# A four-layer graph transformer on one core: layernorm taken apart and run inside the product ahead of it

## The chip, the cores and the metric

The kernel runs on one core of a Trainium2 chip. Its time is the device time of that core for one launch, in microseconds; three runs are given by their median. One further execution was taken by the hardware profiler, and every duration of a single step below comes from that one. The engines are called as in the profile: PE multiplies matrices (PEld loads its stationary operand), DVE is the vector engine, ACT the scalar engine, POOL is GpSimd, and SP sends for most of the transfers.

## The reference, cut to what matters

```python
# x: 512 tokens x 768 features, float32; edges: 16384 (src, dst)
for layer in range(4):
    xn = layernorm(x)                       # (x - mean) / sqrt(var + eps)
    x = x + gnn[layer](xn, edges) + mix[layer](xn)
    x = x + ffn[layer](layernorm(x))
# gnn: graph attention with 8 heads, then 1 (layers 0, 1); graph convolution (2, 3)
# mix[0](xn): y = layernorm(xn) * g1 + b1;  xn = xn + performer(y) @ proj_w + proj_b
#             y2 = layernorm(xn) * g2 + b2; xn + gelu(y2 @ fc1_w + b) @ fc2_w + b   (3072 wide)
# mix[1](xn): linear attention on layernorm(xn) * g + b, then @ w_proj
# mix[2](xn): linear attention, then @ Wo;   mix[3](xn): as mix[0] with linear attention, eps 1e-8
# ffn: 0: mixture of 8 experts of 192 and a shared one; 1: small classifier on 6 tokens with an MLP;
#      2: 3 experts of 1536 and a shared one; 3: 8 experts of 192, 64 tokens each
```

So layernorm over 768 features stands behind a sum into the residual and ahead of the next matrix product some dozen times.

## The kernel before, in words

The tokens are split into four tiles of 128 (`NT` = 4, index t), the features into six chunks of 128 (`KC` = 6, index k). A matrix that a product contracts over features is held feature-major (`xT`), and the residual `x`, and in layers 0 and 3 also `xn`, token-major. A scheduler turns the program into one instruction list for each engine, and decides when a buffer of a pool is handed over.

Every large product is done by Strassen's method in Winograd's form: seven half-size products, each on a half of the tokens and features. The sums of the left operand (`SplitA`, four of them, `s[1]` to `s[4]`) are made on DVE by `all_sums` (L391), where the third, `s[3]` of the code's numbering or buffer `st[2]`, is made on POOL in three pieces (L396); for hidden layers POOL makes all of them (L382 to L385). The differences of the weight (`SplitB`, `t[1]` to `t[4]`) are made on POOL by twelve operations, L411 to L414 for each of three k. `ready` (L398) loads a weight and splits it. The room for weights is a pool of two buffers, later two pools: `w_tile` (L121) takes every third tile from the last pool, the rest from the first, whichever buffer there comes free first. The room for differences has two buffers as well.

`strassen_add` (L543) adds a product into the residual. For each of two halves m of the token tiles it forms banks x, y and z in PSUM and adds them to token tiles m and 2 + m as they come (L583 `add_part`, L821 `add`). The second half of the work for m is `held` and run by `flush`, so that it lies behind the next stage's first products. With `fresh` the product a22·t4 is formed early, in bank x. Which tiles are finished when is fixed by this order: token tiles 0 and 2 first, then 1 and 3.

After the sum a layernorm follows (`normed` L276, `layernorm` L210, `layernorm_chunk` L217), tile by tile in the order 0, 2, 1, 3: two `bn_stats` (L221), an aggregate (L222), a square root on ACT (L225), a reciprocal (L226), three steps of a Newton correction (L229 to L231), and the apply over 768 features (L232). When tiles 0 and 1 are there, `half(0)` of `transposer` (L234) turns them feature-major: twelve PE transposes (L246) and six times two evacuations on ACT and DVE (L202, L204, L254, L257). The second half and `all_sums` are called by the next product once its first parts are under way.

In layer 0 the performer's projection (`proj`) and the first weight of the MLP (`up`, fc1) are made ready while attention runs; `residual_and_mlp` (L817) does the projection with `strassen_add(As, wp, add, True)`, the norm y2, and `mlp` (L793), whose five groups go up and down. Before the performer the normed input is read back from DRAM, normed again, given the projection's bias on POOL and written to a DRAM copy `kept_xn0`. The shared expert of layer 0's mixture is done after the last group's weights are asked for. In layer 1 a tile called `room` is held in one of the weight buffers while the attention heads run, and the last graph attention, whose edges are made by `last_edges` (L1363), lies behind the projection `w_proj`.

## Time and profile before

| what | value |
|---|---|
| median of three runs | 3228.47 us (3226.35 to 3235.73) |
| profiled execution | 3229.27 us, its span 3227.6 us |
| PE busy | 3094.6 us, 96% of the span, 12097 matmuls and transposes |
| DVE, POOL, ACT busy | 1524.1, 1461.4, 637.7 us |
| share of 16 DMA engines | 22.7% |
| mean clock granted to PE | 0.981 |

The profiled execution is 0.8 us above the median and its span leaves 1.7 us around it, so sums made in the profile carry over. The time of an engine's group in the profile is followed by the idle time just ahead of it and by what ended that idle time, written as an arrow with engine, buffer and line. In a timeline row the columns are start, duration, engine, line, operation, out<-in, shape and count; the bracket at its end is the idle time before it and its releaser. A float32 matmul appears as two rows. Idle time of an engine that is not the bound costs nothing.

### The profile page before, as it was taken

The page shows a single profiled execution, that of the slowest core. Times are in us where ns is not written, and L with a number is a line of the kernel's source. Part 1 is how long each engine was busy: PE and PEld are TensorE (multiplying, and loading weights), DVE is VectorE, ACT ScalarE, POOL GpSimd, SP SyncE. Part 2 cuts the span into 40 slices and gives each one's busy share as a digit, 9 for nine tenths or more (in the row PEclk, how much of TensorE's full clock was granted, in tenths as well). Part 3 has the DMA queues.
Part 4 walks back from the last instruction along what each step waited for, and adds up shares of the span by engine and source line. Part 5 has one row for each costly group of instructions (what it writes and reads, how often), then busy time and mean ns, then how long its engine had stood idle before and what let it go on. Part 6 is the DMA issues. An engine that isn't in the chain of part 4 may idle for free.

```text
span 3227.6 us, 32219 instructions
## 1 busy us (share of the span) xinstructions
PE 3094.6 (96%) x12097; PEld 2066.8 (64%) x12097; DVE 1524.1 (47%) x3433; ACT 637.7 (20%) x1268; POOL 1461.4 (45%) x1560
## 2 busy tenths in 40 slices
PE   8999999999999999999998999999999999999999
PEld 3445555555765776765684357777777775677755
DVE  7574444445446324446676535433333336453241
ACT  0132222222252110201441212100000001121101
POOL 0344444445225564464534254355555557355520
PEclk9999999999999999999999999999999999999999
DMA  3021221112202122321111422122222222131221
GB/s 111 14 79 69 69 69 69 69 69 108 88 30 93 59 101 76 108 94 68 45 67 68 119 82 98 59 88 88 89 88 88 89 86 84 70 108 59 89 97 59
DMA packets 92837, 255.23 MB, mean 79 GB/s; under 512 B 9905, under 2 KB 14897, under 8 KB 91530
## 3 DMA queue, kind: packets, MB, share of 16 engines
q1 hardware_dynamic: 92682, 253.18, 22.7%
q8 instruction: 95, 1.56, 0.2%
q14 instruction: 60, 0.49, 0.0%
HBM read 244.23 MB, written 8.93 MB: 78 GB/s over the span
## 4 chain that ended last, share of the span: by engine, by line
PE 81%; DVE 9%; POOL 4%; issue 3%; ACT 1%; DMA 0%; SPq 0%; POOLq 0%; DVEq 0%; ACTq 0%
PE ps L461 39%; PE ps L553 22%; PE ps L751 4%; PE ps L614 3%; PE ps L302 3%; DVE st_u L664 2%; PE ps L922 1%; PE ps L909 1%; PE ps L246 1%; DVE edge_w L637 1%; DVE edge_w L639 1%; POOL tw L411 1%; POOL w L412 1%; POOL tw L413 1%; PE ps L1711 1%
## 5 line engine op out<-in xcount | busy, mean ns | idle before, releaser
L411 POOL TENSOR_TENSOR tw<-w 128x384 f32<-128x384 f32 x246 | 249.9, 1025 | 1094.0 <-PE ps L461 324.0
L461 PE MATMUL ps<-sx,tw 128*128 128x256 f32 x1188 | 304.8, 381 | 3.3 <-DVE sx L393 2.3
L461 PE MATMUL ps<-sx,w 128*128 128x256 f32 x1188 | 293.2, 383 | 0.8 <-DVE room L1264 0.8
L553 PE MATMUL ps<-tw,sx 128*128 128x384 f32 x720 | 252.3, 489 | 9.6 <-POOL tw L413 5.8
L412 POOL TENSOR_TENSOR w<-w 128x384 f32<-128x384 f32 x246 | 253.0, 1036 | 8.5
L413 POOL TENSOR_TENSOR tw<-w 128x384 f32<-128x384 f32 x246 | 252.4, 1033 | 9.5
L414 POOL TENSOR_TENSOR tw<-w,tw 128x384 f32<-128x384 f32 x246 | 250.3, 1024 | 9.9
L553 PE MATMUL ps<-w,sx 128*128 128x384 f32 x720 | 252.5, 486 | 0.0
L461 PEld LDWEIGHTS ps<-sx,w 128*128 128x128 f32 x1188 | 227.4, 192 | 34.5 <-DVE room L1264 1.5
L461 PEld LDWEIGHTS ps<-sx,tw 128*128 128x128 f32 x1188 | 226.4, 191 | 35.4 <-PE ps L461 3.4
L553 PEld LDWEIGHTS ps<-tw,sx 128*128 128x128 f32 x720 | 136.1, 190 | 106.5 <-POOL sx L383 8.0
L583 DVE TENSOR_TENSOR x<-x,ps 128x384 f32<-128x384 f32 x218 | 116.1, 552 | 185.9 <-PE ps L553 185.7
L553 PEld LDWEIGHTS ps<-w,sx 128*128 128x128 f32 x720 | 136.8, 190 | 92.8
L504 DVE TENSOR_TENSOR st_u<-st_p,ps 128x256 f32<-128x256 f32 (+1 forms) x127 | 57.1, 450 | 271.9 <-PE ps L461 271.9
L477 ACT COPY st_p<-ps 128x256 f32<-128x256 f32 (+1 forms) x127 | 50.2, 395 | 667.5 <-PE ps L461 665.6
L461 PE MATMUL ps<-xfT,w 128*128 128x256 f32 x720 | 180.2, 389 | 0.1
L461 PE MATMUL ps<-tw,sx 128*128 128x384 f32 x456 | 166.7, 499 | 14.0 <-DVE st_u L499 6.0
L751 PE MATMUL ps<-edge_wT,h 128*128 128x512 f32 x384 | 168.0, 594 | 8.7 <-DVE edge_wT L204 8.7
L499 DVE TENSOR_TENSOR st_u<-st_p,ps 128x256 f32<-128x256 f32 (+1 forms) x127 | 57.1, 450 | 246.8 <-PE ps L461 143.0
L461 PE MATMUL ps<-w,sx 128*128 128x384 f32 x456 | 160.5, 489 | 1.0 <-DVE ps L505 1.0
L461 PEld LDWEIGHTS ps<-xfT,w 128*128 128x128 f32 x720 | 140.2, 195 | 24.2 <-ACT st_p L477 0.3
L553 PE MATMUL ps<-w,hid 128*128 128x384 f32 x432 | 143.1, 487 | 0.0
(460 smaller groups left out, 5093.3 us busy)
## 6 DMA issues: line engine op xcount, KB each, us to landing
w<-in_L_gnn_W SPq DMA_DIRECT2D x60, 768.0 KB, 6.2
w<-in_L_mix_fc_w SPq DMA_DIRECT2D x48, 768.0 KB, 6.9
row<-in_rows SPq DMA_DIRECT2D x39, 384.0 KB, 3.6
w<-in_L_mix_qkv_w SPq DMA_DIRECT2D x18, 768.0 KB, 7.3
w<-in_L_ffn_w SPq DMA_DIRECT2D x18, 768.0 KB, 6.7
w<-in_L_ffn_routed_gate SPq DMA_DIRECT2D x18, 768.0 KB, 6.0
w<-in_L_ffn_routed_up SPq DMA_DIRECT2D x18, 768.0 KB, 5.9
w<-in_L_ffn_routed_down SPq DMA_DIRECT2D x18, 768.0 KB, 6.0
```

The lines of the kernel that those rows point to most:

```text
L302: T.matmul(ps, parts[k][:, ts(t, P)], w_of(k)[:, ts(c, HC)], start=k == 0, stop=k == n - 1)
L411: G.tensor_sub(tt[:, 0, k], b22[:, k], b12[:, k])
L412: G.tensor_sub(b12[:, k], b12[:, k], b11[:, k])
L413: G.tensor_sub(tt[:, 1, k], b22[:, k], b12[:, k])
L414: G.tensor_sub(tt[:, 2, k], b21[:, k], tt[:, 1, k])
L461: T.matmul(bank, l, r, start=start and k == 0, stop=stop and k == KC // 2 - 1, skip_group_check=True)
L499: V.tensor_add(b["u2"], b["p1r"], b["y"])
L553: T.matmul(b[name], l[:, k, ts(m, P)], r[:, k, :], start=start and k == 0, stop=k == KC // 2 - 1, skip_group_check=True)
L583: V.tensor_add(x[:, t, ts(j, HC)], x[:, t, ts(j, HC)], ps)
L614: T.matmul(acc[t], oh[:, 1, ts(t, P)], oh[:, 0, :], start=j == 0, stop=j == EC - 1)
L664: V.scalar_tensor_tensor(junk, h[:, t, :], 1.0, r, op0=ALU.mult, op1=ALU.mult, accum_out=sc[:, t : t + 1])
L751: T.matmul(ps, h[:, s, ts(f, P)], wT[:, s, :], start=s == 0, stop=s == NT - 1)
```

## The change: what it does

The class `Norm` takes the place of `normed`. Its `part(t, c)` makes the `bn_stats` of half a token tile, and after the second half of a tile `finish(t)` runs the rest of the chain with the same steps as before; `first()` and `rest()` transpose the two halves. `strassen_add` gets a parameter `then`. With it the products come in another order, in which token tiles 0 and 1 receive their last add first, every final add of a half tile is followed by its `bn_stats`, and nothing is held back; the transposes of the first half follow the last product. The `fresh` form is gone from it. The norm is given to `strassen_add` at the projection of layers 0 and 3 (y2), at the last `down` product of both MLPs (the norm of the expert layers), at the end of the experts of layers 0 and 2, and at layer 2's `Wo`. The adds of layer 1's graph attention and classifier call `part` as well, and performer's norm runs tile by tile inside the last `aggregate`.

`all_sums` makes its third sum on DVE in one operation. The bias of the projection is added to `xn` on POOL after the features of the keys instead of before the copy, and the copy is dropped. The shared expert of layer 0 is split: its first products stand between the first `strassen_add` and the second half of group 1, its last ones ahead of the last `strassen_add`. The weight buffers are given out in a fixed turn (a, b, later c, a, b), and a tile that is `held`, layer 1's `room`, leaves the turn until it is given back.

```diff
-    wpools = []
-    taken = [0]
-    def open_weights(bufs):
-        p = tc.tile_pool(name="weights", bufs=bufs, side="right")
-        wpools.append((p, p.__enter__()))
-        taken[0] = 0
-    open_weights(2)
-    def w_tile(name="w"):
-        taken[0] += 1
-        i = len(wpools) - 1 if taken[0] % 3 == 1 else 0
-        return wpools[i][1].tile([P, KC * D], FP, tag="w", name=name)
+    wpools, turns = [], []
+    def open_weights(names):
+        p = tc.tile_pool(name="weights", bufs=1, side="right")
+        wpools.append(p)
+        pool = p.__enter__()
+        turns[:0] = [(pool, n) for n in names]
+    open_weights("ab")
+    def w_tile(name="w", held=None):
+        pool, n = turn_ = turns.pop(0)
+        (turns if held is None else held).append(turn_)
+        return pool.tile([P, KC * D], FP, tag="w" + n, name=name)
...
-    def layernorm(src, dst, eps, order=range(NT), then=None):
-        for t in order:
-            layernorm_chunk(src, dst, eps, t)
-            if then:
-                then(t)
-    def layernorm_chunk(src, dst, eps, t):
...
+    class Norm:
+        def __init__(self, src, name, eps, gain=None, bias=None, sums=True, inplace=False):
+            self.src, self.eps = src, eps
+            self.n = src if inplace else token_major(name)
+            self.T, self.split, self.half = transposer(name + "T", gain, bias, sums)
+            self.st, self.seen = {}, {}
+        def part(self, t, c):
+            if t not in self.st:
+                self.st[t] = tiny(2, 6, name="ln_st")
+                self.seen[t] = 0
+            V.bn_stats(self.st[t][:, c, :], self.src[:, t, ts(c, HC)])
+            self.seen[t] += 1
+            if self.seen[t] == 2:
+                self.finish(t)
+        def chunk(self, t):
+            for c in range(2):
+                self.part(t, c)
+        def finish(self, t):
+            eps = self.eps
+            mv = tiny(2, name="ln_mv")
+            V.bn_aggr(mv, self.st[t].rearrange("p a b -> p (a b)"))
...
+            V.tensor_scalar(self.n[:, t, :], self.src[:, t, :], mean, rs, op0=ALU.subtract, op1=ALU.mult)
+        def first(self):
+            self.half(self.n, 0)
+        def rest(self):
+            self.half(self.n, 1)
...
-    def normed(src, name, eps, gain=None, bias=None, sums=True, order=(0, 2, 1, 3)):
-        xn = token_major(name)
-        dst, split, half = transposer(name + "T", gain, bias, sums)
-        if not sums:
-            layernorm(src, xn, eps, order, by_halves(xn, half))
-            return xn, dst
-        layernorm(src, xn, eps, order, lambda t: half(xn, 0) if t == 1 else None)
-        return xn, dst, split, lambda: half(xn, 1)
...
         def all_sums(self):
             self.eng.tensor_add(self.st[:, 0], self.a21, self.a22)
             self.eng.tensor_sub(self.st[:, 1], self.st[:, 0], self.a11)
+            self.eng.tensor_sub(self.st[:, 2], self.a11, self.a21)
             self.eng.tensor_sub(self.st[:, 3], self.a12, self.st[:, 1])
-            for k in range(KC // 2):
-                G.tensor_sub(self.st[:, 2, k], self.a11[:, k], self.a21[:, k])
...
-    def strassen_add(A, B, add, fresh=False):
+    def strassen_add(A, B, add, then=None):
         banks = [{}, {}]
@@ -555,25 +556,44 @@
             tick()
             return b[name]
+        def plain():
+            for n in range(2):
+                ps = product(n, "x", A.a11, B.b11, True)
+                for i, j in ((0, 1), (1, 0), (1, 1)):
+                    add(2 * i + n, j, ps)
+            for n in range(2):
+                add(n, 0, product(n, "x", A.a12, B.b21, False))
+                if then:
+                    then(n, 0)
+        if then:
+            plain()
+            flush()
+            for m in range(2):
+                add(m, 1, product(m, "y", A.s[2], B.t[2], True))
+            for m in range(2):
+                add(2 + m, 1, product(m, "z", A.s[1], B.t[1], True))
+                add(m, 1, product(m, "z", A.s[4], B.b22, False))
+                then(m, 1)
+            for m in range(2):
+                add(2 + m, 1, product(m, "y", A.s[3], B.t[3], False))
+                then(2 + m, 1)
+            for m in range(2):
+                add(2 + m, 0, product(m, "y", A.a22, B.t[4], False))
+                then(2 + m, 0)
+            return
         def chunk(m):
             def first():
                 if m == 0:
-                    for n in range(2):
-                        ps = product(n, "x", A.a11, B.b11, True)
-                        for i, j in ((0, 1), (1, 0), (1, 1)):
-                            add(2 * i + n, j, ps)
-                    for n in range(2):
-                        add(n, 0, product(n, "x", A.a12, B.b21, False))
-                    if fresh:
-                        for n in range(2):
-                            add(2 + n, 0, product(n, "x", A.a22, B.t[4], True))
+                    plain()
                 add(m, 1, product(m, "y", A.s[2], B.t[2], True))
                 add(2 + m, 1, product(m, "z", A.s[1], B.t[1], True))
                 add(2 + m, 1, product(m, "y", A.s[3], B.t[3], False))
             def second():
                 add(m, 1, product(m, "z", A.s[4], B.b22, False))
-                add(2 + m, 0, banks[m]["y"] if fresh else product(m, "y", A.a22, B.t[4], False))
+                add(2 + m, 0, product(m, "y", A.a22, B.t[4], False))
...
+    def performer_norm():
+        y = token_major("y")
+        nc.sync.dma_start(y, raw_xn)
+        return Norm(y, "y", 1e-5, "m0_g1", "m0_b1", inplace=True)
+
+    def performer_values(n):
 
         B = ready(qkv[:, 2 * D :])
-        xn = token_major("xn")
-        nc.sync.dma_start(xn, raw_xn)
-        _, _, ys, rest = normed(xn, "y", 1e-5, "m0_g1", "m0_b1")
-        add_row_to(xn, row("m0_p"))
-        nc.sync.dma_start(kept0, xn)
+        n.first()
...
-        values(ys, B, row("m0_v"), lambda t, c: va[c][:, t, :, 0:3:2, :], rest)
+        values(n.split, B, row("m0_v"), lambda t, c: va[c][:, t, :, 0:3:2, :], n.rest)
...
+                if norm and n < NT:
+                    norm.chunk(n)
...
-                strassen_add(pending[1], down, add_part)
+                n = None
+                if g == 4:
+                    if after:
+                        after()
+                    n = norm()
+                strassen_add(pending[1], down, add_part, n and n.part)
             else:
                 early()
             pending = g, sums
-        flush()
-
-    def residual_and_mlp(As, wp, eps, g2, b2, w1, f1, w2, f2, func, xn, after=None, kept_in=None):
+        n.first()
+        return n
...
-        strassen_add(As, wp, add, True)
-        flush()
-        _, _, ys, rest = normed(xn, "y2", eps, g2, b2)
+        n = Norm(xn, "y2", eps, g2, b2)
+        strassen_add(As, wp, add, n.part)
+        n.first()
...
         kT = performer_features(ys, 1)
+        add_row_to(xn, row("m0_p"))
...
+        stages = up_part(0)
+        next(stages)
+        pending = next(stages)
+        stages = up_part(1)
+        next(stages)
+        strassen_add(pending, ready(a["L0_ffn_w2"][:D, :]), add_part)
+        flush()
...
         pg, pu = feature_product(wi, xfT, 0), feature_product(wi, xfT, P)
         glu(hid[:, 0, :], pg, pu)
         ps = feature_product(wi, xfT, 2 * P)
         glu(hid[:HD, 1, :], ps[:HD], ps[HD:])
-        strassen_add(pending[1], last, add_part)
-        flush()
+        pending = next(stages)
+        last = ready(a["L0_ffn_w2"][D:, :])
+        gat_w1 = ready(a["L1_gnn_W1"])
+        n1 = Norm(x, "xn", 1e-5)
         token_product([hid[:, 0, :], hid[:HD, 1, :]], lambda k: (w2a, w2b)[k], add_to_x)
+        strassen_add(pending, last, add_part, n1.part)
+        n1.first()
...
-        room = w_tile("room").rearrange("p (i n) -> p i n", n=N)
+        holding = []
+        room = w_tile("room", holding).rearrange("p (i n) -> p i n", n=N)
...
+                nf.part(t, c)
+        turns.extend(holding)
...
-    strassen_add(As, wo, add_part, True)
-    flush()
-    _, xfT, xs, rest = normed(x, "xf", 1e-5)
+    nf = Norm(x, "xf", 1e-5)
+    strassen_add(As, wo, add_part, nf.part)
+    nf.first()
```

## The prediction

> **What bounds the kernel now.** I read the page's busy times first, then its chain of waits, then TensorE's groups with the idle time ahead of each, then the timeline of single stages.
>
> ```profile
> PE 3094.6 (96%) x12097; PEld 2066.8 (64%) x12097; DVE 1524.1 (47%) x3433; ACT 637.7 (20%) x1268; POOL 1461.4 (45%) x1560
> PE 81%; DVE 9%; POOL 4%; issue 3%; ACT 1%; DMA 0%; SPq 0%; POOLq 0%; DVEq 0%; ACTq 0%
> ```
>
> TensorE (PE) is the bound: it idles 3227.6 − 3094.6 = 133 us in all. No other engine is half busy, so a change that removes no product can win only from these 133 us and from matmuls that run slowly around them. Where the idle time lies (last columns: what it waited for):
>
> ```profile
> L246 PE MATMUL ps<-ident,xn 128*128 128x128 f32 x120 | 16.1, 280 | 4.8 <-DVE xn L232 4.2 <-DVE ln_nw L229 0.5
> L246 PE MATMUL ps<-ident,y 128*128 128x128 f32 x96 | 15.6, 313 | 14.8 <-DVE y L232 13.4 <-DVE ln_rs L231 1.4
> L246 PE MATMUL ps<-ident,xf 128*128 128x128 f32 x96 | 14.1, 292 | 12.9 <-DVE xf L232 12.9
> L553 PE MATMUL ps<-w,aT 128*128 128x384 f32 x96 | 36.8, 525 | 5.4 <-DMA w<-in_L_mix_w_proj 4.8 <-DVE xn L821 0.5
> L461 PE MATMUL ps<-tw,sx 128*128 128x384 f32 x456 | 166.7, 499 | 14.0 <-DVE st_u L499 6.0 <-POOL sx L396 5.7 <-DVE sx L393 2.2
> ```
>
> The transposes (L246) behind a layernorm wait 32.5 us for its last step, the apply L232. One such stage, layer 3's y2, on PE and then in windows (PE, PEld, DVE, ACT, POOL busy; granted clock; DMA):
>
> ```profile
> 2886.20 4.03 PE L553 MATMUL ps<-w,sx 128*128 128x384 f32 x12
> 2893.64 0.88 PE L246 MATMUL ps<-ident,y 128*128 128x128 f32 x6 [3.41 <-DVE y L232]
> 2896.25 1.54 PE L246 MATMUL ps<-ident,y 128*128 128x128 f32 x6 [1.74 <-DVE y L232]
> 2897.59 7.43 PE L461 MATMUL ps<-y2T,w 128*128 128x256 f32 x24
> 2906.69 2.86 PE L461 MATMUL ps<-y2T,tw 128*128 128x256 f32 x12 [0.36 <-DVE y2T L254]
> 2910.39 1.53 PE L461 MATMUL ps<-sx,tw 128*128 128x256 f32 x6 [0.84 <-DVE sx L393]
> ```
>
> ```profile
> 2882.00:2890.00 8.00, 8.00 (x26) 4.56 (x24) 5.44 (x13) 0.24 (x2) 4.74 (x6) 1.00 0.00 0
> 2890.00:2898.00 8.00, 2.86 (x14) 2.19 (x14) 7.59 (x25) 1.81 (x7) 8.00 (x8) 0.80 0.82 288
> 2898.00:2906.00 8.00, 8.00 (x35) 6.73 (x35) 1.03 (x3) 3.90 (x8) 5.17 (x6) 0.77 0.02 7
> 2906.00:2911.00 5.00, 3.80 (x19) 2.88 (x17) 4.80 (x8) 0.97 (x3) 2.09 (x3) 1.00 0.00 0
> ```
>
> The product's last add is followed by statistics, a chain of small steps and two applies; PE stands 6.35 us in four gaps. Then the clock is 0.80 and 0.77, so a gap costs twice. Counting each matmul's excess over the median of its group (here 3.6 us), this stage loses 9.95 us. Such losses, gaps and excess, over all of PE (us): start of layer 0: 3.6; performer y 8.8; layer 0's y2 9.1; xf 6.7; start of layer 1: 11.3; its projection 15.2; its xf 4.5; start of layer 2: 7.0; its xf 8.9; start of layer 3: 8.0; second norm .3; y2 9.95; last xf 2.3. Sum 95.7. The rest of the 133 (routers, sorting, layer 1's edges) is untouched.
>
> The 15.2 are not a norm:
>
> ```profile
> 1722.15 1.41 SPq L156 DMA_DIRECT2D w<-in_L_mix_w_proj  x3
> 1726.95 4.54 PE L553 MATMUL ps<-w,aT 128*128 128x384 f32 x8 [4.83 <-DMA w<-in_L_mix_w_proj]
> 1736.33 0.91 PE L553 MATMUL ps<-tw,sx 128*128 128x384 f32 x2 [2.58 <-POOL tw L413]
> 1740.50 1.65 PE L553 MATMUL ps<-tw,sx 128*128 128x384 f32 x2 [3.26 <-POOL tw L413]
> ```
>
> The weight is sent for at 1722.15, when the buffer before it is let go; PE waits for it, then twice for POOL's differences, and runs slowly for 4.5 us.
>
> **The change, part by part.**
>
> *Norm by parts.* A product in `strassen_add` is three matmuls of 0.672 us, 14 products about 28.3 us. In the new order tokens 0 and 1 get their last add (z, s4·b22) before ten more matmuls, 6.7 us. Their chain there: add .55, bn_stats .56, aggregate .2, square root .29, reciprocal .15 and three small steps of .2, with the hand-overs about 1.55, two applies at the slow 1.30: 5.3 us, under 6.7. So the first twelve transposes follow the last matmul directly. Tokens 2 and 3 take the same 5.3 us after the end; ahead of PE lie 12 transposes (1.5) and nine to twelve matmuls of 0.448 (4.0 to 5.4), 5.5 to 6.9. What is left is the wait for DVE's sums of the transposed half (two sums of .94 ahead of the wanted one): 1.5 to 1.8 a stage. No bn_stats is added; where `fresh` stood 18 adds replace 20, 1.1 us less DVE. DVE's work beside the product is 18 × .46 + 8 × .5 + 4 × 2.2 = 21 us of 28.3, so it keeps up.
>
> *all_sums.* Three POOL operations of .72 become one on DVE of about .95. Two prices speak: on DVE it comes first and can hold the next sums by .95; on POOL it sat behind row adds (5.7 us of waits in the group above). At the start of layer 2 POOL's is the gap of 4.17; it goes.
>
> *Rule against trace, ports.* The apply took 1.30 and L392 1.39 beside POOL work, .68 and .95 apart from it. The Trainium skill, SBUF — State Buffer, "Who interferes with whom", says that a VectorE instruction with two SBUF inputs, or a copy or tensor_scalar in a 2-port mode, is locked out for a whole GpSimd operation. That speaks against laying the norm beside the split of the next weight (1.0 us an operation). By the rule in full, four applies would wait 4 × 1.0 more a stage, 44 us over eleven; by the rows, +.62, already in the 5.3. I take the rows.
>
> *Rule against trace, clock.* The same skill, TensorE: Matmul & The Clock Gate, Part 1, gives half clock after one idle window of about 3.4 us until one busy window: an estimate of 1.7 us lost a stage. The rows show 2.5 to 3.7. With gaps cut to 1.8 us both say that the loss goes; by the rule the sum would be about 10 us smaller over ten stages. I take the rows.
>
> *Two stages with a new wait.* At layer 2's xf and layer 3's y2 the a22 products stood early as cover; now s2·t2 follows the first products, and DVE does four sums (3.7 us) ahead of the adds that free the banks. 1.7 to 2.5 us; I take 2.5.
>
> *Buffers, layer 0.* Before, the projection's weight was sent for at 892.64 and split at 899 to 912; fc1's at 997.96, split from 1003.96. With fixed turns the projection gets the slot that is free last. Its 12 split operations (1.0 each) then begin near 1004 and alternate with fc1's: PE stands about 3.3 + 1 us for differences and 1.5 for the transfer, and loses 2.5 by the clock. That is +7.5 to 8.3 and eats what y2 gains (9.1 − 1.8). Net 0, bounds −3 (it fits) and +4.
>
> *Buffers, layer 1.* The projection gets q's slot, done near 1675: transfer 6 us, split 12 us, ready about 1694, 28 us ahead of need. 14 of the 15.2 go; bound 10, if the row adds on POOL come first.
>
> *The rest.* Start of layer 1: the second norm waits 1 to 3 us more behind reduces while one reduce fewer stands before L499; gain 3, bounds 0 and 7. The moved shared expert issues the same matmuls; gat_w1 now loads after it, 7 + 12.4 us beneath a 28.3 us product. Dropping the round trip of xn saves two 1.5 MB transfers nobody waits for. The row add to xn (8 × .96 = 7.7 us) moves to POOL's idle 10.49 us ahead of 894.80. These cost nothing while that cover stands; without it 1 to 3 us each.
>
> **Sum.** Gains: 3 + 6.2 + 0 + 4.9 + 3 + 14 + 1 + 5.5 + 4.6 + 6.3 + 5.6 + .3 + 1.5 = 55.9. The profiled execution took 3229.27 (span 3227.6 and 1.7 around it), .8 above the median 3228.47. So 3229.3 − 55.9 = 3173.4, on the median 3172.6. I say 3174.
>
> **The rivals.**
> 1. Waits come back (.22). If sums first and slow applies leave 3.4 us a stage, not 1.7, PE still drops its clock: 1.7 + 1.0 back at each of ten stages, 27 us: about 3201. For: DVE is 7.59 of 8 busy in the bad window. Against: the chain fits by 1.4 us.
> 2. Only the buffers pay (.08): the scheduler reorders the adds so that the norm still comes last. 3228.5 − 14 = 3214. Against: the instruction order of the changed kernel, laid beside the old, keeps the adds and statistics as written.
> 3. Slower (.05): fixed turns. A weight must now take its own slot, not whichever comes free first. There are 246 / 3 = 82 split weights; each late one stops PE. To cross to slower by .3% it must cost (55 + 9.7) / 82 = .8 us a weight. At 1.0 each: 3256. For: the layer 0 case. Against: elsewhere the order of the transfers hardly moves, and the product of 28 us hides 18 to 20 us of load and split.
> 4. It does nothing, gains at stages given back at layers 0 and 1 (.03): 3226.
>
> **How the numbers follow.** Forecast .62, own range 3155 to 3192 (its bounds: layer 1's start ±4, layer 0 ±4, the projection −4, three quarters of a microsecond at ten stages). The range 3150 to 3206 adds most of rival 1. A measurement here tells .3%, 9.7 us, from no change: the forecast, rival 1 and rival 2 are faster: .92; same .03; slower .05.
>
> **What would show it.** In the profile after: PE idle near 98 us (35 of the gain is gaps) and busy about 3074 (21 is slow matmuls); L246's waits for L232 from 32.5 to under 8; windows after a product's end at clock .95 or more; no gap on the layer 1 projection and its issue near 1675 less the time won; gaps for L413/L414 of 3 us in layer 0's projection. Wrong, if the transposes still wait over 3 us, if L553 waits for weights at many places, or if DVE is over 55% busy.

## The result, and the profile after

| | median (range), us | profiled execution, its span |
|---|---|---|
| before | 3228.64 (3226.35 to 3235.73) | 3229.27, 3227.6 |
| after | 3206.02 (3205.90 to 3208.21) | 3206.01, 3204.3 |

The ratio is 0.9928, with a 95% interval of 0.9911 to 0.9945. (A fourth execution of the kernel before moves its median from 3228.47 to 3228.64.) The change wins 22.6 us where 55 were forecast: it is faster, by less than half of what the sum said, and 3206.02 lies at the upper end of the range 3150 to 3206.

The page after, first the busy times, then the chain that ended last by engine:

```profile
PE 3082.3 (96%) x12087; PEld 2060.9 (64%) x12097; DVE 1540.6 (48%) x3442; ACT 635.4 (20%) x1266; POOL 1430.0 (45%) x1515
PE 83%; DVE 10%; POOL 3%; issue 2%; ACT 1%; DMA 0%; SPq 0%; POOLq 0%; DVEq 0%; ACTq 0%
```

PE's idle time went from 133 to 3204.3 − 3082.3 = 122 us and its busy time from 3094.6 to 3082.3: 11 us of gaps and 12 of busy time were won, where 35 of gaps and 21 of slow matmuls were forecast. So 24 of the 33 us that are missing are gaps that stayed or came. PE's groups after (last columns: idle time ahead, and what ended it):

```profile
L461 PE MATMUL ps<-sx,tw 128*128 128x256 f32 x1188 | 306.7, 383 | 9.5 <-DVE sx L394 8.5 <-DVE st_u L499 1.0
L554 PE MATMUL ps<-tw,sx 128*128 128x384 f32 x720 | 253.7, 490 | 13.2 <-DVE sx L394 5.3 <-POOL sx L384 4.1 <-POOL tw L413 3.8
L554 PE MATMUL ps<-tw,aT 128*128 128x384 f32 x48 | 19.2, 554 | 5.3 <-DVE xn L854 5.3
L267 PE MATMUL ps<-ident,xn 128*128 128x128 f32 x120 | 15.5, 273 | 1.2 <-DVE xn L247 1.2
L267 PE MATMUL ps<-ident,xf 128*128 128x128 f32 x96 | 12.9, 283 | 3.8 <-DVE xf L247 3.8
L267 PE MATMUL ps<-ident,y 128*128 128x128 f32 x96 | 12.1, 273 | 0.0
L461 PE MATMUL ps<-w,xnT 128*128 128x384 f32 x312 | 112.9, 501 | 9.4 <-ACT st_p L477 8.7 <-ACT xnT L202 0.5
```

The transposes' wait for the apply (now L247) is 1.2 + 3.8 + 0 = 5.0 us instead of 30.5 (the 32.5 of the prediction are all waits of the transposes; 1.9 of them were for steps ahead of the apply): the norm did move off PE's path. In its place stand waits for DVE's sums (L394), one of 5.3 for a residual add (L854), one of 3.8 for the differences (L413), and 8.7 for a PSUM copy on ACT (L477), 7.28 of it in one place.

The stage that the prediction showed, layer 3's y2, on PE, and two windows of it (sum, then PE, PEld, DVE, ACT, POOL busy; granted clock; DMA share and GB/s):

```profile
2868.32 4.03 PE L554 MATMUL ps<-tw,aT 128*128 128x384 f32 x12
2872.19 1.47 PE L267 MATMUL ps<-ident,y 128*128 128x128 f32 x12
2877.98 1.47 PE L267 MATMUL ps<-ident,y 128*128 128x128 f32 x12
2885.06 1.53 PE L461 MATMUL ps<-sx,tw 128*128 128x256 f32 x6 [1.72 <-DVE sx L394]
```

```profile
2870.00:2876.00 6.00, 5.74 (x29) 4.08 (x28) 5.54 (x15) 2.45 (x7) 4.79 (x6) 1.00 0.63 251
2876.00:2884.00 8.00, 7.34 (x40) 6.22 (x39) 6.69 (x13) 4.02 (x7) 8.00 (x7) 1.00 0.00 0
```

Both dozens of transposes run with no gap ahead of them, the clock is 1.00 where it was 0.80 and 0.77, and one wait of 1.72 for a sum is left.

The buffers at layer 1's projection (w_proj), on SP's queue and on PE:

```profile
1678.72 1.43 SPq L156 DMA_DIRECT2D w<-in_L_mix_w_proj  x3
1727.69 4.03 PE L554 MATMUL ps<-w,aT 128*128 128x384 f32 x12
1731.56 0.81 PE L554 MATMUL ps<-tw,sx 128*128 128x384 f32 x2
```

The weight is sent for 49 us ahead of its use, and the three gaps are gone.

How much each stage took is read from the starts of like PE instructions in both traces. A stage is named by the norm or product in it; y2 is the norm ahead of an MLP, xf the one ahead of the experts or the classifier. In us won, with a minus for lost and the forecast in brackets: start of layer 0 2.2 (3); performer y 8.05 (6.2); **layer 0's projection with y2 −8.75 (0)**; its xf 2.05 (4.9); **start of layer 1 −5.2 (3)**; **layer 1's middle −3.7 (not foreseen)**; its w_proj 15.5 (14); its xf −.2 (1); start of layer 2 3.4 (5.5); its xf 3.1 (4.6); start of layer 3 5.2 (6.3); second norm −.5 (.3); y2 4.7 (5.6); **last xf −2.4 (1.5)**. They sum to 23.4, against 23.3 by the spans. Four stages, in bold, are 25 us short of their terms; the rest is 8 short in small pieces.

### The profile page after: what moved, and what is told of

Its sections match the earlier page's. It is cut to its first block, busy times and chain, and to the rows that moved or that the text cites. A ratio compares the mean times of both kernels' runs of the same rounds, so it can differ in the third digit from the quotient of the medians.

```text
span 3204.3 us, 32139 instructions
## 1 busy us (share of the span) xinstructions
PE 3082.3 (96%) x12087; PEld 2060.9 (64%) x12097; DVE 1540.6 (48%) x3442; ACT 635.4 (20%) x1266; POOL 1430.0 (45%) x1515
## 4 chain that ended last, share of the span: by engine, by line
PE 83%; DVE 10%; POOL 3%; issue 2%; ACT 1%; DMA 0%; SPq 0%; POOLq 0%; DVEq 0%; ACTq 0%
PE ps L461 40%; PE ps L554 23%; PE ps L776 4%; PE ps L301 3%; PE ps L634 3%; DVE st_u L684 2%; PE ps L291 1%; PE ps L943 1%; PE ps L267 1%; PE ps L1769 1%; DVE edge_w L657 1%; PE ps L1433 1%; PE ps L346 1%; DVE edge_w L647 1%; DVE edge_w L659 1%
## 5 line engine op out<-in xcount | busy, mean ns | idle before, releaser
L413 POOL TENSOR_TENSOR tw<-w 128x384 f32<-128x384 f32 x246 | 255.3, 1045 | 9.6
L477 ACT COPY st_p<-ps 128x256 f32<-128x256 f32 (+1 forms) x127 | 50.2, 395 | 643.9 <-PE ps L461 641.7
L499 DVE TENSOR_TENSOR st_u<-st_p,ps 128x256 f32<-128x256 f32 (+1 forms) x127 | 57.2, 450 | 245.7 <-PE ps L461 144.8
```

The source lines that it names most:

```text
L413: G.tensor_sub(tt[:, 1, k], b22[:, k], b12[:, k])
L499: V.tensor_add(b["u2"], b["p1r"], b["y"])
```

## The experiments

Each kernel is the changed one with one edit, unless the text says otherwise. The ratio is to the kernel before, with its 95% interval. A stage that "wins" is compared with the same stage of the changed kernel, read from the starts as above, in one trace of each.

### Layer 0's projection and y2: two causes, a late weight and a lock

A lock is here short for one engine standing still inside an instruction for as long as another works. The trace after shows both causes. First the sending of the weight, before and after:

```profile
892.64 1.39 SPq L156 DMA_DIRECT2D w<-in_L_mix_proj_w  x3
```

```profile
988.09 1.39 SPq L156 DMA_DIRECT2D w<-in_L_mix_proj_w  x3
```

Then PE, and DVE with POOL:

```profile
1003.18 4.21 PE L554 MATMUL ps<-tw,sx 128*128 128x384 f32 x6 [3.78 <-POOL tw L413]
1030.04 6.88 PE L554 MATMUL ps<-tw,aT 128*128 128x384 f32 x12 [5.34 <-DVE xn L854]
1050.58 1.53 PE L461 MATMUL ps<-sx,tw 128*128 128x256 f32 x6 [2.22 <-DVE sx L394]
```

```profile
1020.42 4.82 POOL L316 TENSOR_TENSOR x<-x,row 128x384 f32<-128x384 f32 x5
1023.22 6.23 DVE L247 TENSOR_SCALAR y<-xn,ln_mv,ln_rs 128x768 f32<-128x768 f32 x1
1025.18 3.85 POOL L865 TENSOR_TENSOR x<-x,xn 128x384 f32<-128x384 f32 x4
1031.90 0.81 DVE L247 TENSOR_SCALAR y<-xn,ln_mv,ln_rs 128x768 f32<-128x768 f32 x1
```

The weight is sent for 95 us later than before, so PE waits 3.78 for its differences. Later the first apply takes 6.23 us, where another takes 0.81. It begins within a row of POOL operations without a break and ends .42 after the row does (1029.45 and 1029.03). The residual adds that free the banks are behind it in DVE's order, so PE waits 5.34 for one of them. The row itself ends because POOL's next add, at 1030.13, waits for DVE again.

**Buffers alone** (the kernel before, with the fixed turns and with the held tile taken out of them):

> Before, with only the buffers of the change: fixed turns for the weights, and the tile that layer 1 holds taken out of the turn. Norms, sums and products are as before. Theory (the buffers carry a gain in layer 1 and a loss in layer 0 of their own): the wait for layer 1's projection goes, 14 to 16 us; layer 0's projection is sent for near 998 instead of 892 and PE loses 5 to 8 us there: 3229 - 15 + 7 = about 3221. Rival (the 15 us in layer 1 need the new place of the shared expert or of the norm as well): the wait stays, and the time is 3229 or more.

Measured 3226.25 (3222.47 to 3228.69), ratio 0.9987 (0.9980 to 0.9993). Against the kernel before, layer 1's projection wins 15.5 and layer 0's loses 13.9, both read from the starts. So in the kernel before the turns cost almost what they win, in another place, and the time is 5 us longer than expected. PE in layer 0:

```profile
1015.97 3.62 PE L552 MATMUL ps<-tw,aT 128*128 128x384 f32 x6 [5.90 <-POOL tw L413]
1023.59 2.92 PE L552 MATMUL ps<-tw,aT 128*128 128x384 f32 x4 [4.00 <-POOL tw L413]
```

**The turns of layer 0 swapped**, so that the projection gets the slot that is free first:

```diff
+        turns.reverse()
         proj = ready(a["L0_mix_proj_w"])
```

> After, with one thing undone: layer 0's projection and fc1 change places in the two weight slots, so that the projection's weight goes again to the slot that is free about 110 us earlier. Theory (the fixed turn makes the weight late): the issue of the projection's weight moves back from 988 to near 883, its split from 993-1006 to before 905, PE's gaps of 0.59 and 3.78 us in that product go, and with the slow matmuls behind them the stage ends 5 to 7 us earlier: about 3200. The gap of 5.34 us at the end of that product, for which a long apply on DVE stands, stays at 4 to 6 us if it comes from POOL's row of additions, which this edit does not remove. Rival (the product was late for another reason, for instance DVE's reciprocal of 3.35 us and the additions queued behind it): the stage ends no more than 2 us earlier, and the time stays within 2 us of 3206.

Measured 3193.68 (3192.44 to 3197.47), ratio 0.9894 (0.9877 to 0.9910). The stage wins 12.0, more than expected: the gaps for the weight are gone, and with the product earlier the apply begins when POOL's row is nearly over, so it is short and the gap of 5.34 is gone too.

```profile
1013.79 3.85 POOL L865 TENSOR_TENSOR x<-x,xn 128x384 f32<-128x384 f32 x4
1016.76 1.29 DVE L247 TENSOR_SCALAR y<-xn,ln_mv,ln_rs 128x768 f32<-128x768 f32 x1
```

The apply still ends .41 after POOL's row (1018.05 and 1017.64).

**The row adds elsewhere**: only the lock is to go, the late weight stays.

```diff
         add_row_to(xn, row("m0_p"))
+        add_row_to(x, row("m0_f2"))
...
-            add_row_to(x, row(f2))
+            if not kept_in:
+                add_row_to(x, row(f2))
```

> After, with one thing moved: the eight additions of fc2's bias to x, which POOL did back to back beside layer 0's projection (1020 to 1025 us), are issued before the performer's features, in POOL's idle time of 10.5 us there. Theory (a two-port apply on DVE is shut out for as long as POOL's unbroken row of two-input additions lasts): the apply that took 6.23 us takes under 2 us, the gap of 5.34 us ahead of the last twelve matmuls of the projection falls under 1 us, and the stage ends 4.5 to 6 us earlier: about 3201. Rival (the apply was long for a reason of its own, such as a wait that the record does not show): it still takes over 5 us and the time is as before, 3206.

Measured 3198.47 (3195.97 to 3200.20), ratio 0.9905 (0.9890 to 0.9919). The apply takes 0.98, the gap of 5.34 is gone, and the stage wins 10.5; the waits for the weight stay (3.57 + .64).

```profile
1018.21 4.04 POOL L866 TENSOR_TENSOR x<-x,xn 128x384 f32<-128x384 f32 x4
1021.68 0.98 DVE L247 TENSOR_SCALAR y<-xn,ln_mv,ln_rs 128x768 f32<-128x768 f32 x1
```

The row is shorter, and the apply again ends .41 after it: 1022.66 against 1022.25.

**The row made longer**: eight more adds on POOL behind the row (four of them take off again what the first four put on).

> After, with eight more additions on POOL (half of the bias added to x a second time and taken away again) behind the row of bias additions in layer 0, about 7.7 us more of an unbroken row. In three runs the first apply of that norm ended 0.41 to 0.42 us behind the end of POOL's row, whenever it had begun. Theory (the apply is shut out until the row ends): it grows from 6.2 to about 13.9 us, again ends about 0.4 us behind the row, PE's gap of 5.34 becomes about 13, and the time is 3206 + 7.7 = about 3214. Rival (DVE gets in between two of POOL's operations and the 6.23 us have another cause): the apply stays at 5 to 7 us and the time within 2 us of 3206.

Measured 3215.04 (3214.92 to 3217.29), ratio 0.9959 (0.9943 to 0.9975). DVE's apply, the end of POOL's row, and PE:

```profile
1024.65 14.66 DVE L247 TENSOR_SCALAR y<-xn,ln_mv,ln_rs 128x768 f32<-128x768 f32 x1
1035.06 3.84 POOL L870 TENSOR_TENSOR x<-x,xn 128x384 f32<-128x384 f32 x4
1039.91 5.37 PE L554 MATMUL ps<-tw,aT 128*128 128x384 f32 x10 [13.78 <-DVE xn L854]
```

One DVE instruction of 14.66 us, ending .41 after the row (1039.31 and 1038.90); PE stands 13.78 behind it, and the kernel is 9 us longer. The 6.23 was thus no property of the apply: its length follows POOL's row. Six more of the kernels below keep the late weight and the row, and in the trace of each this apply is as long: 7.06 to 8.02, ending .41 to .42 after the row.

### Start of layer 1: two small things, neither enough alone

PE after, then ACT and DVE ahead of it:

```profile
1492.39 5.47 PE L461 MATMUL ps<-w,xnT 128*128 128x384 f32 x10 [7.28 <-ACT st_p L477]
```

```profile
1491.68 0.29 ACT L240 ACTIVATE ln_rs<-ln_mv,epsc 128x1 f32<-128x1 f32 x1 [1.93 <-DVE ln_mv L237]
1491.88 0.46 ACT L477 COPY st_p<-ps 128x384 f32<-128x384 f32 x1
1486.01 2.27 DVE L1220 TENSOR_REDUCE deg<-cnt 128x4 f32<-128x2048 f32 x1
```

PE needs the PSUM bank that ACT's copy (L477) empties. PE filled its last bank by 1485.1, and ACT stood idle for 1.93 us ahead of 1491.68 without making the copy: ahead of the copy in its list is the second norm's square root, which waits for statistics from a full DVE, where the row sums of the edge counts (`deg`) take 2.27. Two suspects: ACT's order and DVE's load.

**The square root off ACT.** For this one norm, whose input is normed already, rs = 1.5 − .5 (var + eps) on DVE, close to the inverse root where var is near 1, takes the place of root, reciprocal and correction:

```diff
+            if self.unit:
+                V.tensor_scalar(rs, var, eps, -0.5, op0=ALU.add, op1=ALU.mult)
+                V.tensor_scalar(rs, rs, 1.5, None, op0=ALU.add)
```

> After, with the second norm of layer 1 alone done without ACT: since its input is normed already, the inverse root starts from 1 and takes one Newton step on DVE, so that ACT's four square roots, the reciprocals and two small steps of each tile are gone. Theory (ACT works in order, and its copy of the first bank, on which PE waits 7.28 us at 1485, is queued behind the second norm's square roots, which wait for a full DVE): the gap of 7.28 falls to 2 us or less, and the stage ends 4 to 7 us earlier: about 3200. Rival (DVE itself is the bound of that stage, at 100% from 1473 to 1494): PE stops a little later for DVE instead, at the transposes of the second half or for the sums, and the gain is under 2 us: 3204 to 3206.

Measured 3205.56 (3201.24 to 3210.08), ratio 0.9927 (0.9912 to 0.9942). The stage wins .9 by its end (2.2 at 1500, right behind the waits), not visible in the total. PE's 7.28 becomes three waits; besides one of .77 they are:

```profile
1492.65 0.41 PE L272 MATMUL ps<-ident,xn 128*128 128x128 f32 x2 [1.96 <-DVE ln_rs L242]
1495.69 4.21 PE L466 MATMUL ps<-w,xnT 128*128 128x384 f32 x6 [1.31 <-ACT st_p L482]
```

**The row sums moved** to layer 0, ahead of the last graph attention there, the norm as in the kernel after (the copy into `deg` only makes the sum wait for `h2`):

```diff
+        deg = const.tile([P, NT], FP, name="deg")
+        V.tensor_copy(deg, h2[:, :, 0])
+        V.tensor_reduce(deg, cnt, AX.X, ALU.add)
         qT = last_gat(h2,
...
-        V.tensor_reduce(deg, cnt, AX.X, ALU.add)
```

> After, with only the counts' row sums (2.27 us on DVE, first needed in layer 2) made in layer 0 instead of at the start of layer 1; the second norm keeps its square roots on ACT. With both edits PE stood nowhere for 0.4 us in the stage and it ended 9.4 us earlier, with the norm's alone 2.7. Theory (DVE's total is the bound, and the row sums stand ahead of the square root that ACT's copy st_p waits behind): the gap of 7.28 falls to about 3 to 4 and the stage ends 4 to 6 us earlier: about 3201. Rival (ACT's order is the cause and DVE only a part of it): the gap stays at 5 us or more and the gain is 2.3 at most: 3204.

Measured 3216.40 (3215.40 to 3220.64), ratio 0.9963 (0.9950 to 0.9976): slower than the kernel after. At layer 1 it wins .8 and the gap is still 6.61. About 8 us are lost far from the edit, at the start of layer 0, where PE has a gap of 8.82; DVE and POOL ahead of it:

```profile
136.45 12.27 DVE L395 TENSOR_TENSOR sx<-xnT 128x768 f32<-128x768 f32 x1
145.96 1.94 POOL L414 TENSOR_TENSOR tw<-w,tw 128x384 f32<-128x384 f32 x2
```

The same sum took 1.71 in the kernel after, beside the same split on POOL:

```profile
136.20 1.71 DVE L395 TENSOR_TENSOR sx<-xnT 128x768 f32<-128x768 f32 x1
136.10 2.67 POOL L413 TENSOR_TENSOR tw<-w 128x384 f32<-128x384 f32 x2
```

In one case both engines take turns and each is slower; in the other DVE stands until POOL's row is over (147.90; the sum ends at 148.72).

**Both together:**

> After, with the second norm of layer 1 done without ACT as in the run before, and the row sums of the graph's counts (2.27 us on DVE, first needed in layer 2) made in layer 0 instead of at the start of layer 1. The run with the norm alone turned one wait of 7.28 us into three of 1.96, 0.77 and 1.31 and slow matmuls, and won 2 us in the stage. Theory (DVE, without a pause from 1473 to 1495, is the bound at the start of layer 1): another 2.3 us off DVE is another 2 to 3 us off the stage: 4 to 5 us in all, about 3202. Rival (ACT's or PE's order keeps the stage): no more than the 2 us of before: 3204 to 3206.

Measured 3202.21 (3199.25 to 3202.89), ratio 0.9907 (0.9893 to 0.9922). The stage wins 8.2 by its end (9.4 at 1500), and no gap of .4 or more is left in the stretch shown. The same stretch of time after, and with both edits:

```profile
1472.00:1496.00 24.00, 16.72 (x66) 10.56 (x65) 21.59 (x66) 5.47 (x16) 16.14 (x15) 0.87 0.16 66
```

```profile
1472.00:1496.00 24.00, 23.62 (x107) 15.64 (x106) 22.99 (x67) 7.77 (x19) 15.43 (x15) 1.00 0.16 66
```

PE is busy 23.62 of 24 us instead of 16.72, at clock 1.00 instead of .87, with DVE busy 22.99 instead of 21.59. The two together win far more than their parts (.9 + .8): each alone leaves the other's wait standing. In six kernels with neither edit this stage loses between 4.5 and 5.5, so the .9 and .8 are hardly clear of chance; the 8.2 is.

### The third sum

After the change PE waits for L394, the sum that follows the third one on DVE, in six places: 2.22, 2.41, 2.81, 2.19, 2.47 and 1.72 us. The third sum is not needed first.

**Back on POOL**, in three pieces as before:

> After, with the third sum of the left operand (st[2]) back on POOL in three pieces. Theory (on DVE it is done first and holds the sums that PE waits for): the six waits of PE for the sum L394, 2.22, 2.41, 2.81, 2.19, 2.47 and 1.72 us, shrink by about 0.9 us each, 5 us in all, and 1 to 2 us come back in layer 1 and at the start of layer 2, where POOL has its row additions and splits: about 3202. Rival (the move was worth its price: POOL's pieces come late, as the gap of 4.17 us before the change showed): the start of layer 2 loses 3 us or more and the time is 3206 to 3210.

Measured 3206.93 (3206.06 to 3207.62), ratio 0.9931 (0.9916 to 0.9946). The six waits fall to .57, .85, 2.27, .52, 1.53 and 1.02, and three waits of 1.36 and one of 1.46 for POOL's sums take their place. In layer 1's middle it wins 1.4. The net is nothing.

**On DVE, but last**, made from the second sum:

```diff
-            self.eng.tensor_sub(self.st[:, 2], self.a11, self.a21)
             self.eng.tensor_sub(self.st[:, 3], self.a12, self.st[:, 1])
+            self.eng.tensor_sub(self.st[:, 2], self.a22, self.st[:, 1])
```

> After, with the third sum made from the second one (a22 - s2 in place of a11 - a21, the same value), still on DVE: it can then not be done ahead of the sums that PE waits for. The run with that sum on POOL showed the wait for L394 cut from about 2.2 to 0.6 us at three stages and a wait of 1.36 us for POOL's sum right behind it. Theory (only the order on DVE costs): the six waits for L394 fall by about 0.9 us each, with no new wait for the third sum, since three products of 2 us lie before it: 4 to 6 us in all, about 3201. Rival (the price is DVE's total, the sum is waited for where it comes): PE waits for the third or fourth sum instead and the time is within 2 us of 3206.

Measured 3202.20 (3199.46 to 3204.58), ratio 0.9909 (0.9894 to 0.9924): about 4 us less than the kernel after, as expected. The six waits fall to .57, .85, 2.22, .53, 1.53 and none; none comes for the third sum, but four of .66 to 1.08 for an add on DVE (L499) do.

### The last xf

The clock in the routers' stretch at the end, after and before:

```profile
3102.00:3109.00 7.00, 6.23 (x30) 6.12 (x29) 1.68 (x6) 2.63 (x5) 0.00 (x0) 0.50 0.00 0
```

```profile
3126.00:3132.00 6.00, 5.31 (x44) 5.21 (x44) 1.34 (x5) 1.88 (x4) 0.00 (x0) 0.86 0.70 164
```

After, the clock is .50 while PE counts as busy 6.23 of 7 us with small matmuls. **The last norm as it was before**, after the whole product:

> After, with the last norm alone (layer 3's experts) as before the change: the last product in the old order, the norm behind it tile by tile. In the change this stage ended 2.3 us later than before, though PE's gaps there went from 2.1 to 1.9 us; its router's light matmuls (8 columns) ran in the window 3102 to 3109 at clock 0.50, where they had 0.86 before. Theory (the new order sends 24 of these light matmuls ahead of the second half's transposes, the clock drops, and the other 24 run at half speed): the clock in that window is back to 0.8 or more and 2 to 2.5 us come back: about 3204. Rival (the loss is of the order of the adds themselves): the clock stays near 0.5 or the time does not change by more than 0.5 us in that stage.

Measured 3206.35 (3205.03 to 3207.29), ratio 0.9930 (0.9913 to 0.9946). The stage loses 1.6 instead of 2.4, and the clock in that window is .62: less than was expected, more than the rival allowed. The 46 light matmuls in the old order took 6.59 us in one row, where the kernel before took 5.61. In the thirteen other traces with the new order this stage loses 2.4 to 4.1, so the order seems to cost .8 us or more; the other 1.6 stays open.

### All repairs in one kernel, twice

Swapped turns, row adds elsewhere, third sum last, norm without ACT, row sums moved:

> After, with all repairs together: the projection and fc1 of layer 0 in each other's weight slot, the bias additions moved to POOL's idle time, the third sum last on DVE, layer 1's second norm without ACT, and the counts' row sums in layer 0. The swap alone gave 12.4 us and the moved additions 7.6; both act on the same stage, which lost about 13 us in all beside what a free stage loses, so together they give 13. With 4 to 6 for the sum and 4 to 5 for layer 1: about 3206 - 22 = 3184. Rival (the swap alone had already freed the apply on DVE, and the sum's wait moves on): 3190 to 3193.

Measured 3184.31 (3176.75 to 3186.22), ratio 0.9849 (0.9834 to 0.9865), its profiled span 3175.0. That it meets the expected 3184 is in part luck, as the repeat below shows. In that trace layer 0's projection with y2 is 5.7 us better than the kernel before, not 8.75 worse, and the start of layer 1 is 2.8 better, not 5.2 worse. Layer 1's middle (−3.9) and the last xf (−4.1) stay lost.

**The same with s1·t1 ahead of s2·t2**, so that the sums are wanted later:

> The version with all repairs, and one more: in the product that carries a norm, s1*t1 of both halves goes ahead of s2*t2, so that DVE's second sum has 4 us of cover more. The version with all repairs still waits 2.28 us at layer 2's xf and 1.57 at layer 3's y2 for that sum. Theory (PE meets the sums in the order in which DVE makes them): both gaps fall under 0.3 us and the time is 3 to 4 us less than the 3184 of that version: about 3181, its profiled span from 3175 to about 3171. Rival (the last adds of tokens 0 and 1 come no later, but banks come free later): the gaps move to the adds and the gain is under 1 us.

Measured 3186.79 (3185.56 to 3191.86), ratio 0.9871 (0.9856 to 0.9886). The waits at layer 2's xf and layer 3's y2 fall from 2.28 to 1.04 and from 1.57 to nothing; the one at layer 3's start grows from 1.09 to 1.98. Two losses are not of this edit, for the repeat below, which lacks it, shows them too: a wait of 3.43 in layer 0 behind a DVE multiply of 4.28 (1.40 in the trace of all repairs), and the sum at the start of layer 0, which takes 12.25. So the totals don't settle what the edit is worth.

**The kernel of all repairs again**, beside **the same with the third sum first**:

> The version with all repairs once more, the same kernel. Its first four times were 3176.75, which is the profiled one and in which no sum on DVE was longer than 1.75 us at the start of layer 0, and 3183.12 to 3186.22. In two other kernels of this study one sum there took 12.27 and 12.25 us, to the end of POOL's row of splits, and PE waited 8.8 and 7.6 us. Theory (the same lock-out happens there in some executions of one kernel and not in others): the times fall into two groups about 8 us apart, near 3177 and 3185, and the profile shows a sum of about 12 us at 135 us if its own time is in the upper group, and none if in the lower. Rival (the 3176.75 is a chance value): one group around 3184, and a profile with no such sum at a time over 3182.

> All repairs but one: the third sum is first on DVE again, as in the change. Theory (that order costs about 0.4 to 0.9 us at six stages, as the kernel with the sum alone moved won 4): 3 to 4 us more than the version with all repairs, so about 3180 in executions without a shut-out sum at the start of layer 0 and 3188 with one. Rival (once the other waits are gone the sum has cover): within 1.5 us of the version with all repairs, group by group.

Measured 3194.20 (3192.58 to 3200.57), ratio 0.9894 (0.9878 to 0.9911), and 3196.99 (3190.80 to 3200.64), ratio 0.9896 (0.9881 to 0.9911). With the third sum first the six waits are back (2.35, 2.54, 2.96, 1.37, 2.62, 1.85), but the median is only 2.8 higher, within the spread: here the order of the sum shows no difference in the total. And one kernel has two medians 10 us apart, with ranges that don't meet, while the kernel before is at 3229.83 and 3230.26 beside them. The times did not fall into the two groups that were expected, 3177 and 3185; the shut-out sum did come back, as the theory had it for a long time. The same DVE sum in its two profiled executions, the first of 3175.0 us, the second of 3192.3:

```profile
135.94 1.69 DVE L398 TENSOR_TENSOR sx<-xnT 128x768 f32<-128x768 f32 x1
```

```profile
137.41 12.21 DVE L398 TENSOR_TENSOR sx<-xnT 128x768 f32<-128x768 f32 x1
```

The start of layer 0 is 7.6 of the 17.3 us between the two, and a DVE multiply of 4.30 us in layer 0, also beside POOL, 2.9 more; the rest lies in small steps. So whether the engines alternate or DVE is shut out at this sum is not fixed by the program: the same kernel shows both. What decides it is not shown. At its first median this version is the shortest of all that ran; at its second, 3194, it is 12 us shorter than the change and no better than the swapped turns alone (3193.68).

## Why the prediction was right or wrong, point by point

By the spans 23.3 us came of 55.9. Three terms of the sum that were taken as 0, 3 and nothing (layer 0's projection with y2, the start of layer 1, its middle) came out at −8.75, −5.2 and −3.7; the last xf fell 3.9 short, and the other stages 8 in small pieces. The main idea, that the norm leaves PE's path, held. What failed was the price of the moved work on the other engines.

- **"Rule against trace, ports … I take the rows": the step that failed most clearly.** The rows chosen, 1.30 against .68, came from places in the trace where DVE and POOL alternate. The Trainium skill, SBUF — State Buffer, "Who interferes with whom", states that the one that issues first gets the shared ports for the whole instruction and the other blocks fully. Here the block was real and longer than that sentence says: not one POOL operation of 1.0 but the rest of the unbroken row, 6.23 and, with a longer row, 14.66. The rule in full at every apply (44 us) was wrong too; all other applies of the trace after take 1.49 at most. It needed a third case: where does an apply start within an unbroken POOL row, with PE's bank behind it? In layer 0 the adds `x += xn` and the row adds stand right there, which can be read from the order of the instructions; that DVE would stand for all of them could not. Price: the gap of 5.34, and 10.5 for the stage.
- **"Buffers, layer 0 … Net 0, bounds −3 and +4": its mechanism right, its surroundings not.** A projection that gets the slot free last, its split interleaved with fc1's, is in the trace (issue 988.09). In the kernel before the buffers alone cost 13.9 and not 7.5 to 8.3, with gaps for differences of 5.90 and 4.00 and not 3.3 and 1. In the changed kernel one of 3.78 is left of them; with the late weight left and only the row of adds moved, the stage is 1.75 better than before, within the bounds. So it is the lock on top that makes it −8.75. The two repairs overlap: 12.0 or 10.5 alone, 14.5 in the kernel of all repairs.
- **"Start of layer 1 … gain 3, bounds 0 and 7": wrong sign, −5.2.** The prediction looked at the norm's waits on DVE. It missed the queue behind the square root: ACT's PSUM copy, which PE needs. A root of 0.29 us that waited for a full DVE stood ahead of it, and PE waited 7.28. Only with the root gone and DVE unloaded did the stage come back, by 8.2.
- **Layer 1's middle (−3.7) was not in the sum.** At its end three PSUM copies on DVE stand between four sums of 1.41 to 2.56 beside POOL's row adds, and PE waits 1.57, .70 and .76 for them. Moving the third sum to POOL gave 1.4 back; the rest is not settled.
- **"All_sums … on DVE it comes first and can hold the next sums by .95": named, and sized low.** "1.5 to 1.8 a stage" was 1.72 to 2.41. The two prices it weighed do cancel, as the sum back on POOL showed: no net. A third way, on DVE but last, was not weighed; it took 4 us off.
- **The two stages with a new wait: right.** 2.5 each was taken; 2.81 and 2.47 are in the trace.
- **Buffers, layer 1: right.** 14 forecast, 15.5 measured, and the same 15.5 with the buffers alone. The issue was expected at 1675 less the time won; 3.65 had been lost by then, and it came at 1678.72.
- **Norm by parts: right in its mechanism.** The transposes' waits are 5.0 ("under 8"), and the clock stays 1.00 after layer 3's y2; which of the two readings of the clock sized that gain rightly is not shown. The performer's y won 8.05 where 6.2 was forecast; the starts of layers 2 and 3, their xf and y2 won 16.4 of 22.0.
- **The last xf (1.5 forecast, −2.4 measured)**: the clock of .50 is in the trace; undoing the norm's new order gave .8 back. The rest is open.
- **The rivals.** The number of rival 1, 3201, is the nearest of all, but by luck: its mechanism, clock lost at ten stages, is not what happened. Three stages lose 17.7 us between them, by waits that no rival named. Rivals 2 and 4 are refuted by the transposes' waits. Rival 3 needed late weights at many places; a late weight stopped PE in one.

## What to carry to other kernels

When work is moved beside a product, ask of each moved instruction what stands behind it in its engine's order and who waits for that: here PE waited 7.28 us for a copy behind a tiny root in ACT's queue, and 5.34 for an add behind one apply in DVE's. Keep a DVE instruction whose successor PE needs away from a long unbroken row on POOL, or put the row somewhere else; moving the row adds won 10.5 us in its stage, beside the 22.6 of the whole change. And what a fixed turn of buffers is worth differs at each use: in the kernel before the same turns won 15.5 us at one weight and lost 13.9 at another. Reversing them once in the changed kernel kept the first and won 12.0 at the second.

## What the runs showed of the hardware that was not expected

A DVE instruction can be shut out for a whole row of POOL operations. For a tensor_scalar of 128x768 (the next one of its kind took .81) it was 6.23 us and, with eight more POOL operations, 14.66; beside this row of adds it was so in all eight traces that have the late weight and the row, and it ended .41 to .42 us after the row's last operation. For a tensor_tensor of the same size it was 12.21 to 12.36 in four profiles, where it took 1.60 to 1.79 in the twelve others. Two ways of sharing exist: both engines alternate and are slower (the sum 1.7, POOL's operations 1.33 each), or one stands still. The same kernel shows both in different executions, and what chooses between them was not found. One trace of a kernel is little to go by, but all four long sums are in kernels with the row sums moved to layer 0. Six kernel traces have that edit, and the ten without it show none. Whether the edit makes the shut-out more likely was not tested.
